# Table of filter stretches copied in 24 parts on SyncE's queue, one per image of attention; offsets loaded first, padded filters read back on ScalarE's queue

## The chip, the cores and the metric

The kernel runs on one core of one Trainium2 chip. The metric is device time in microseconds (us) of one execution; lower is better. The kernel before takes 10876.6 us, the median of 3 runs (10869.42 to 10882.96). A core has TensorE (PE in the views; PEld is its weight load), VectorE (DVE), ScalarE (ACT), GpSimd (POOL) and SyncE (SP), each with its own in-order stream of instructions, and 16 DMA engines. A DMA is issued by an instruction in the stream of SP, ACT or POOL ("SPq", "ACTq", "POOLq" in the views).

## The reference

Four layers, each of the form x = x + f(normalised x), over 32 images of 192 channels of 56 x 56:

```python
x = x + _L0_conv_ref(_gn(x), ...)   # agent attention, 6 heads, 49 agents
x = x + _L1_conv_ref(_gn(x), ...)   # a recurrent scan (RWKV) over the 3136 pixels
x = x + _L2_conv_ref(_gn(x), L2_conv_offset)   # shift by 48 offsets, 3x3 filter
x = x + _L3_conv_ref(_gn(x), L3_conv_z, ...)   # a long convolution
```

The part that the change touches belongs to the last layer. Its 192 filters of 55 x 55 don't depend on x; a small network of sines makes them from a position code z:

```python
h = jnp.sin(f1 * (einsum('bchw,oc->bohw', z, W1) + b1))
h = jnp.sin(f2 * (einsum('bchw,oc->bohw', h, W2) + b2))
k = einsum('bchw,oc->bohw', h, W3) * (jnp.exp(-distance_map * abs(deltas)) + shift)
y = irfft2(rfft2(x, s) * rfft2(k[0], s), s)[centre] + bias * x
```

and the third layer's 48 offsets are rounded to shifts, with a 3x3 filter for what is left.

## The kernel before, in words

**Stages.** `make_filter` makes the filters; `attention` does layer 0, image by image; `scan_pairs` does layer 1 on pairs of images; `channel_blocks` does layers 2 and 3 channel by channel, with the filters in a table in DRAM. Their order on each engine is made by a scheduler: it gives every instruction a place in its engine's stream, by its own model of times, and so instructions of neighbouring stages and images stand between each other. It can move a DMA issue ahead of code written earlier. What is put under `keep_in_program_order` is fixed behind the instruction that was traced last on the same engine.

**`make_filter`** loads z, weights and the distance map (L255), and calls `beside()`, which loads the first image and the weights of attention (L414 to L426). `_find_shifts` then loads the offsets `off` (L205) and positions `at` (L207), both on SP, and finds the shifts of layer 3 on VectorE (from L208). The sines are made in six rounds of matmul, seven VectorE instructions and one ScalarE instruction (L282 to L291); L317 and L319 make the filters `out` in two halves of 96 channels, and L324 stores each half in DRAM (`filt`). Eight DMAs (L335) write zeros to the ends of the table `lags`. Then six blocks of 32 channels follow: two DMAs read the block from `filt` into one of two `padded` tiles (L350, 55 rows, runs of 220 bytes), TensorE transforms its rows (L360), VectorE and ScalarE copy the result out in two forms, `straight` and `crossed` (L368 to L371), and eight DMAs write these to `lags` (L376, 55 x 8 runs of 336 bytes each). All of these DMAs are issued by SP.

**`copy_spans`** (L382) copies `lags` in DRAM to the table `spans` in DRAM, in the layout of `channel_blocks`: each DMA takes 16 channels and one of the two forms, 2352 KB, issued by GpSimd (L391). `attention` calls it as `beside(b)` for the first 12 images, two DMAs per call, 24 in all. Nothing in attention reads the result, so the scheduler is free to issue them early.

**`attention`**, for one image: statistics and pooled sums of the next image (`moments`: L504, L506, and `by_x`, L513), agents (L567 to L584), then four column groups j of the image. `seen` writes two small tables per image, `gk_c` and `gq_c`, by a DMA from a tile `once` that repeats it (L585, 597.2 KB each, on SP). In the first half `weigh` uses `gk_c` (L651, L652). Between the halves `ask` uses `gq_c`: matmuls L743 and L744 fill a tile in PSUM, VectorE finds a maximum (`mx`, L747) and subtracts it (`pq`, L748), which frees the PSUM tile; ScalarE takes the exponential (L756); VectorE sums and scales (L758 to L760). There are four PSUM tiles for all of it. `join` (L716 to L731) puts the four groups of the first half together, into `values`, with one small ScalarE exponential `f` (L719) in its midst. `turn_back` transposes (L770, copies L774), and `answer` multiplies by `values` (L783, L788). An image ends with stores (L880 to L885).

Tiles of `make_filter` and of attention share memory: the first `by_x` can be written only when the last `lags` DMA has read its source.

Of the kernel before, what the change touches and what calls it, by code (L numbers as in the profile page):

```python
# [20 lines left out]
F32 = mybir.dt.float32  # L21
# [7 lines left out]
C = 192  # L29
# [39 lines left out]
HALF = 64  # L69
FREQ = 2 * NF  # L70
LAGS = 2 * S
SPAN = 8
# [86 lines left out]
def _bc(ap, shape):  # L159

    return ap.unsqueeze(len(ap.shape)).to_broadcast(shape)
# [33 lines left out]
        return mean, rs, nb  # L195


def _find_shifts(nc, cp, a, k, taps):

    NP = C // 4
    found = cp.tile([128, NP, 12], F32, name="found", tag="found")
    off = cp.tile([128, NP, 2], F32, name="off", tag="off")
    nc.sync.dma_start(out=off, in_=a["L2_conv_offset"].partition_broadcast(128))  # L205
    at = cp.tile([128, 2], F32, name="at", tag="at")
    nc.sync.dma_start(out=at, in_=k["chan_k"][:, k["chan_k"].shape[1] - 2 :])  # L207
    nc.vector.tensor_scalar(off, off, -(2.0**21), 2.0**21, ALU.max, ALU.min)  # L208
    rnd = cp.tile([128, NP, 2], F32, name="rnd", tag="rnd")
    nc.vector.tensor_scalar(rnd, off, BIG, None, ALU.add)  # L210
    nc.vector.tensor_scalar(rnd, rnd, BIG, None, ALU.subtract)
    gs = cp.tile([128, NP * 2, 3], F32, name="gs", tag="gs")
    nc.vector.tensor_tensor(off, off, rnd, ALU.subtract)
    flat = off.rearrange("p n d -> p (n d)")
    for f in range(3):
        nc.vector.tensor_scalar(gs[:, :, f], flat, float(f - 1), None, ALU.add)
    nc.vector.tensor_tensor(gs, gs, gs, ALU.mult)
    nc.scalar.activation(gs, gs, AF.Exp, scale=-2.0)
    gsum = cp.tile([128, NP * 2], F32, name="gsum", tag="gsum")
    nc.vector.tensor_reduce(gsum, gs, AX.X, ALU.add)  # L220
    nc.vector.reciprocal(gsum, gsum)
    nc.vector.tensor_tensor(gs, gs, _bc(gsum, [128, NP * 2, 3]), ALU.mult)
    nc.vector.tensor_scalar(rnd, rnd, float(-S), float(S), ALU.max, ALU.min)

    ok, low = (cp.tile([128, NP], F32, name=n, tag=n) for n in ("ok", "low"))
    for i, axis in enumerate((1, 0)):
        nc.vector.tensor_scalar(ok, rnd[:, :, axis], at[:, i : i + 1], None, ALU.add)
        nc.vector.tensor_scalar(low, ok, -0.5, None, ALU.is_gt)
        nc.vector.tensor_scalar(ok, ok, S - 0.5, None, ALU.is_lt)
        nc.vector.tensor_tensor(ok, ok, low, ALU.mult)  # L230
        nc.vector.tensor_tensor(found[:, :, 6 * i : 6 * i + 3], gs[:, axis::2], _bc(ok, [128, NP, 3]), ALU.mult)
        for f in range(3):
            nc.vector.tensor_scalar(found[:, :, 6 * i + 3 + f], rnd[:, :, axis], float(1 - f), None, ALU.add)
    nc.sync.dma_start(out=taps, in_=found)
# [3 lines left out]
def make_filter(ctx: ExitStack, tc: tile.TileContext, a, consts, filt, lags, spans, taps, beside):  # L238
# [4 lines left out]
    nc = tc.nc  # L243
    cp = ctx.enter_context(tc.tile_pool(name="f_c", bufs=1))
# [6 lines left out]
    n = RC * KS  # L251

    def load(name, shape, ap):
        t = cp.tile(shape, F32, name=name, tag=name)
        nc.sync.dma_start(out=t, in_=ap)  # L255
        return t
# [8 lines left out]
    dist = load(  # L265
        "dist", [T, P2], a["L3_conv_distance_map"].rearrange("a b h w -> (a b h w)").partition_broadcast(T)
    )
    beside()
    _find_shifts(nc, cp, a, consts, taps)
    nd = cp.tile([T, 2], F32, name="nd", tag="nd")  # L270
    nc.vector.tensor_scalar(nd, per["deltas"], -1.0, None, ALU.mult)
    nc.vector.tensor_tensor(nd, nd, per["deltas"], ALU.min)
    out = cp.tile([T, 2, P2], F32, name="out", tag="out")
# [21 lines left out]
    for i in range(0, KS // RC, 2):  # L295
        p1 = pp.tile([128, BANK], F32, name="p1", tag="p1")
        for h in range(2):
            c = min(i + h, KS // RC - 1)
# [26 lines left out]


    NI = 16
    f1 = load("f1", list(consts["f1"].shape), consts["f1"])
    none = KH + 1
    zeros = cp.tile([T, (none + 1) * FREQ], F32, name="zeros", tag="zeros")  # L330
    nc.gpsimd.memset(zeros, 0.0)
    for t in range(2):
        for i in range(2):
            for r in (0, LAGS - none - 1):
                nc.sync.dma_start(  # L335
                    out=lags[t * T : (t + 1) * T, i, r : r + none + r % 2].rearrange("c r f -> c (r f)"),
                    in_=zeros[:, : (none + r % 2) * FREQ],
                )
    nc.sync.dma_start(out=spans[C * (S // SPAN) * 128 :], in_=zeros[0:SPAN, 0:FREQ])
    padded = [cp.tile([128, NI, HALF], F32, name=f"padded{i}", tag=f"padded{i}") for i in range(2)]  # L340
# [3 lines left out]
    def psum():  # L344
        return pp.tile([128, BANK], F32, name="ps", tag="ps")

    for c0 in range(0, C, 2 * NI):
        t = padded[c0 // (2 * NI) % 2]
        for i in range(2):
            nc.sync.dma_start(  # L350
                out=t[HALF * i : HALF * i + KS, :, 0:KS],
                in_=filt[c0 + i : c0 + 2 * NI : 2].rearrange("q (a b) -> a q b", b=KS),
            )
        flat = t.rearrange("p q w -> p (q w)")
        got = [wp.tile([128, NI // 2, 2, FREQ], F32, name=n, tag=n) for n in ("straight", "crossed")]
        for g0 in range(0, NI // 2, 3):
            n = min(3, NI // 2 - g0)
            ps = psum()
            for g in range(n):
                nc.tensor.matmul(  # L360
                    ps[:, g * 2 * FREQ : (g + 1) * 2 * FREQ], flat[:, (g0 + g) * 128 : (g0 + g + 1) * 128], f1,
                    start=True, stop=True,
                )
            cos, sin = (
                ps[:, : n * 2 * FREQ].rearrange("p (c m u) -> p c m u", m=2, u=NF)[:, :, m] for m in range(2)
            )
            a0, b0 = (x[:, g0 : g0 + n].rearrange("p g s (u m) -> p (g s) u m", m=2) for x in got)
            nc.vector.tensor_copy(a0[..., 0], cos)  # L368
            nc.scalar.copy(a0[..., 1], sin)
            nc.scalar.mul(b0[..., 0], sin, -1.0)  # L370
            nc.vector.tensor_copy(b0[..., 1], cos)  # L371
        for i, x in enumerate(got):
            for p in range(2):
                for s in range(2):
                    c = c0 + 2 * p + s
                    nc.sync.dma_start(  # L376
                        out=lags[c : c0 + 2 * NI : 4, i, none : none + KS].rearrange("g r f -> r g f"),
                        in_=x[HALF * p : HALF * p + KS, :, s],
                    )


def copy_spans(nc, lags, spans, c):  # L382


    n = S // SPAN
    for i in range(2):
        first = lags[c, i]
        there = bass.AP(first.tensor, first.offset, [[2 * LAGS * FREQ, 16], [SPAN * FREQ, n], [1, HALF * FREQ]])
        first = spans[c * n * 128 + HALF * i]
        here = bass.AP(first.tensor, first.offset, [[n * 128 * FREQ, 16], [128 * FREQ, n], [1, HALF * FREQ]])  # L390
        nc.gpsimd.dma_start(out=here, in_=there)  # L391


def _blocks_of(t, at):
# [4 lines left out]
class _Ready:  # L399
# [19 lines left out]
    def load(self, nc, a, k):  # L419
        self.first = self.image(nc, a, 0)  # L420
        for to, ap in ((self.k, k["att_k"]), (self.w, a["att_w"]), (self.c, a["att_c"])):
            nc.sync.dma_start(out=to, in_=ap)
        for to, ap in ((self.gk_c, a["coef_k"]), (self.gq_c, a["coef_q"])):
            nc.sync.dma_start(out=to[65:KC], in_=ap)
        for j, w in enumerate(WIDTHS):
            nc.sync.dma_start(out=self.xs_c[j][64:KC], in_=k["spread"][:, S * STARTS[j] : S * (STARTS[j] + w)])  # L426
# [1414 lines left out]
@with_exitstack  # L1841
def all_blocks(ctx: ExitStack, tc: tile.TileContext, a, k, out):
    nc = tc.nc
    NB = out.shape[0]
    dp = ctx.enter_context(tc.tile_pool(name="dram", bufs=1, space=DRAM))

    def scratch(name, shape):
        return dp.tile(shape, F32, name=name, tag=name)

    x1, x2 = scratch("x1", [NB, C, N]), scratch("x2", [C, 2, S, NB // 2, S])  # L1850
    filt, rs2 = scratch("filt", [C, KS * KS]), scratch("rs2", [C, 2, 2, NB // 2])
    lags, taps = scratch("lags", [C, 2, LAGS, FREQ]), scratch("taps", [128, C // 4, 12])
    spans = scratch("spans", [C * (S // SPAN) * 128 + SPAN, FREQ])
    st_a, st_c = scratch("st_a", [128, 2, NB // 2, 9]), scratch("st_c", [2, 64, 2, NB // 2, 9])
    with tc.tile_pool(name="a_r", bufs=1) as rp, tc.tile_pool(name="a_x", bufs=2) as xp:
        ready = _Ready(rp, xp)
        make_filter(tc, a, k, filt, lags, spans, taps, lambda: ready.load(nc, a, k))
        attention(
            tc, a, ready, x1, st_a, st_c, lambda b: copy_spans(nc, lags, spans, 16 * b) if b < C // 16 else None
        )  # L1860
    with tc.tile_pool(name="count", bufs=1) as cp:
        count = cp.tile([1, 1], I32, name="count", tag="count")
        scan_pairs(tc, a, k, x1, st_a, st_c, x2, rs2, count)
        n = nc.values_load(count[0:1, 0:1], min_val=0, max_val=128)
        with tc.If(n > 0):
            scan_guarded(tc, a, k, x1, x2, rs2)
    channel_blocks(tc, taps, k, x2, rs2, spans, out)
# [104 lines left out]
```

## Time and profile before

| What | us |
|---|---|
| median of 3 runs | 10876.6 |
| the profiled execution, its own time | 10882.12 |
| its span (first to last instruction) | 10880.3 |
| from the start to the first `by_x` of attention | 322.5 |
| store of one image to store of the next (L883, 656.74 to 803.32) | 146.6 |

Over the span TensorE is busy 88%, VectorE 85%, ScalarE 59%, GpSimd 27%. A page of the profile divides the span in 40 slices of 272 us: TensorE is at two tenths in the first and at nine in nearly all others, and the DMA engines at seven tenths in the first, one tenth through attention and eight to nine in the last quarter. In the views below, a line of waits names the waiting engine and line, what it waited for, and us in total, number of times, the longest. A line of the timeline starts with the start and the duration in us; the square brackets hold the idle time before it and what ended it.

### The profile page before, as it was taken

To read this page: it belongs to the slowest core of one execution; us is meant where nothing else is said; L and a number is where in the kernel's file an instruction comes from. 1 tells how busy PE (TensorE), PEld (TensorE's weight loads), DVE (VectorE), ACT (ScalarE), POOL (GpSimd) and SP (SyncE) were. 2 spreads that over 40 slices of the span, in tenths; PEclk is the share of its full clock that TensorE was granted. 3 is DMA by queue.
4 is the path that set the end of the run, shared out by engine and by line. 5 is a ranking of instruction groups with operands and counts; after the bars stand their busy time and mean duration, and the time that the engine had idled before them with its cause. 6 is when DMAs were issued, how large, how long until landed. Compare 5 with 4: busy or idle time off the path is not lost. (4 is left out here: it accounts for less than half of the span.)

```text
span 10880.3 us, 166788 instructions
## 1 busy us (share of the span) xinstructions
PE 9566.8 (88%) x64806; PEld 5949.0 (55%) x64806; DVE 9238.9 (85%) x11668; ACT 6379.6 (59%) x11966; POOL 2912.6 (27%) x2638
## 2 busy tenths in 40 slices
PE   2799999999999999998788888888888799999998
PEld 1456655555665555564333333333333578777776
DVE  2688888888888888887999999999999577777777
ACT  1455555555555555554666666666666476666666
POOL 0000000000000000001655555555555444444441
PEclk7899999999999999999899999999999899999999
DMA  7311111111111111112333444333333588988888
GB/s 226 121 39 31 43 45 45 45 45 35 35 44 45 45 45 45 31 37 63 82 97 99 100 98 101 102 99 97 97 97 99 152 273 272 274 273 272 275 269 265
DMA packets 1104878, 1240.32 MB, mean 114 GB/s; under 512 B 773091, under 2 KB 807200, under 8 KB 1091992
## 3 DMA queue, kind: packets, MB, share of 16 engines
q1 hardware_dynamic: 1090768, 1146.05, 37.1%
q0 software_dynamic: 3072, 57.80, 1.6%
q10 hardware_dynamic: 10240, 25.70, 0.9%
q8 instruction: 516, 8.45, 0.3%
q14 instruction: 282, 2.31, 0.1%
HBM read 915.94 MB, written 306.43 MB: 112 GB/s over the span
## 5 line engine op out<-in xcount | busy, mean ns | idle before, releaser
L638 DVE SCALAR_TENSOR_TENSOR o<-v_a,att_w,o 128x896 f32<-128x896 f32 (+1 forms) x1024 | 1054.6, 1030 | 422.5 <-ACT v_a L612 295.4
L1155 POOL MEMSET f<- 128x1 f32 x96 | 8.9, 99 | 4730.4 <-DMA st_c<-st 4725.2
L1535 DVE STREAM_TRANSPOSE z<-turned 128x1792 f32<-128x1792 f32 x192 | 677.7, 3529 | 275.9 <-ACT turned L1535 275.7
L1535 ACT COPY y<-ps 64x252 f32<-64x252 f32 (+1 forms) x2304 | 784.0, 340 | 159.8 <-PE ps L1535 130.3
L1148 ACT ACTIVATE q<-q 128x784 f32<-128x784 f32 x384 | 328.4, 855 | 810.5 <-DVE q L1143 635.4
L655 ACT ACTIVATE pr<-ps,low 98x896 f32<-98x896 f32 (+1 forms) x384 | 352.4, 918 | 560.0 <-DVE low L653 560.0
L903 PE MATMUL ps<-sq,fixed 128*128 128x392 f32 x512 | 298.2, 745 | 428.8 <-ACT sq L1226 428.8
L1535 POOL TENSOR_TENSOR xn<-x,scale 128x896 f32<-128x896 f32 x192 | 336.0, 1750 | 1194.9 <-DMA x<-x 704.2
L638 DVE SCALAR_TENSOR_TENSOR o<-v_c,att_w,o 128x448 f32<-128x448 f32 (+1 forms) x1024 | 635.9, 621 | 5.0
L651 PE MATMUL ps<-xs_a,gk_a 128*98 128x448 f32 (+1 forms) x1536 | 638.7, 496 | 0.0
L652 PE MATMUL ps<-xs_c,gk_c 125*98 125x448 f32 (+1 forms) x1536 | 633.3, 493 | 5.4 <-DMA gk_c<-once 5.4
L743 PE MATMUL ps<-gq_a,xs_a 128*112 128x294 f32 x1792 | 602.2, 417 | 19.2 <-DVE pq L748 19.2
L903 PE MATMUL ps<-x,weights 128*128 128x392 f32 x1536 | 573.2, 516 | 28.4 <-DVE bv L1177 14.3
L744 PE MATMUL ps<-gq_c,xs_c 125*112 125x294 f32 x1792 | 594.2, 412 | 0.0
L1535 PEld LDWEIGHTS ps<-toep,y 128*32 128x32 f32 x16896 | 515.0, 151 | 113.4 <-ACT y L1535 107.1
L1535 PE MATMUL ps<-toep,y 128*32 128x112 f32 x16896 | 562.5, 290 | 0.0
L756 ACT ACTIVATE pq<-pq 112x1176 f32<-112x1176 f32 x224 | 265.3, 1184 | 495.3 <-DVE pq L748 372.7
L1535 PE MATMUL ps<-rows,xn 128*112 128x112 f32 x3072 | 378.3, 281 | 151.2 <-POOL xn L1535 151.0
L1535 ACT ACTIVATE turned<-ps,rs 128x448 f32<-128x448 f32 (+1 forms) x576 | 383.5, 666 | 214.1 <-PE ps L1535 207.4
L1535 PE MATMUL ps<-fixed,padded 128*128 128x168 f32 x3072 | 493.5, 316 | 0.0
L1535 PEld LDWEIGHTS ps<-fixed,padded 128*128 128x128 f32 x3072 | 459.7, 197 | 2.4 <-issue 1.9
L903 PEld LDWEIGHTS ps<-sq,fixed 128*128 128x128 f32 x512 | 137.5, 285 | 579.7 <-ACT sq L1226 483.2
(369 smaller groups left out, 25658.8 us busy)
## 6 DMA issues: line engine op xcount, KB each, us to landing
toep<-spans SPq DMA_DIRECT2D x192, 2352.0 KB
x<-x SPq DMA_DIRECT2D x576, 392.0 KB
x<-x SPq DMA_DIRECT2D x896, 196.0 KB
out_x<-done SPq DMA_DIRECT2D x384, 196.0 KB
spans<-lags POOLq DMA_DIRECT2D x24, 2352.0 KB, 50.7
x<-in_x SPq DMA_DIRECT2D x32, 1568.0 KB
x<-x SPq DMA_DIRECT2D x32, 1568.0 KB
x<-in_x SPq DMA_DIRECT2D x64, 392.0 KB
```

The costliest lines, as they stand in the source:

```text
L638: nc.vector.scalar_tensor_tensor(dst, tap(i), dww[:, t, i : i + 1], dst, ALU.mult, ALU.add)
L651: mm(ps[P2, h, :n], g[:, cols], xs_a[j][:, px], start=True, stop=False)
L652: mm(ps[P2, h, :n], gk_c[0:KC, 2 * j + h, cols], xs_c[j][0:KC, px], start=False, stop=True)
L655: nc.scalar.activation(pr[:, :, :n], ps[P2, :, :n], AF.Exp, bias=low[:, j, p : p + 1], accum_out=sums[:, j, p : p + 1])
L743: mm(ps[:SUB, i, :HA], xs_a[j][:, px], g, start=True, stop=False)
L744: mm(ps[:SUB, i, :HA], xs_c[j][0:KC, px], gq_c[0:KC, 2 * j + (q + i) // ns], start=False, stop=True)
L756: nc.scalar.activation(flat, flat, AF.Exp)
L903: mm(out, aa, srcs[t][h], start=True, stop=False)
L1148: nc.scalar.activation(den, den, AF.Ln)
L1155: nc.gpsimd.memset(s, 0.0)
L1535: return lambda *args, **kw: self.tc.keep_in_program_order(do(*args, **kw))
```

## The change

Three edits. The offsets, the positions and the transform matrix `f1` are loaded ahead of `beside()`. The six reads of `filt` are issued by ScalarE instead of SP, two ahead of the loop and each later one behind the matmuls of the block that had the tile before. And `copy_spans` takes one part (16 channels, one form) per call, on SP, fixed in program order, for the first 24 images.

```diff
-    off = cp.tile([128, NP, 2], F32, name="off", tag="off")
-    nc.sync.dma_start(out=off, in_=a["L2_conv_offset"].partition_broadcast(128))
-    at = cp.tile([128, 2], F32, name="at", tag="at")
-    nc.sync.dma_start(out=at, in_=k["chan_k"][:, k["chan_k"].shape[1] - 2 :])
...
+    off = load("off", [128, C // 4, 2], a["L2_conv_offset"].partition_broadcast(128))
+    at = load("at", [128, 2], consts["chan_k"][:, consts["chan_k"].shape[1] - 2 :])
+    f1 = load("f1", list(consts["f1"].shape), consts["f1"])
     beside()
-    _find_shifts(nc, cp, a, consts, taps)
+    _find_shifts(nc, cp, off, at, taps)
...
-    for c0 in range(0, C, 2 * NI):
+    def fetch(c0):
         t = padded[c0 // (2 * NI) % 2]
         for i in range(2):
-            nc.sync.dma_start(
+            nc.scalar.dma_start(
...
+    fetch(0)
+    fetch(2 * NI)
+    for c0 in range(0, C, 2 * NI):
...
+        if c0 + 4 * NI < C:
+            fetch(c0 + 4 * NI)
         for i, x in enumerate(got):
...
-def copy_spans(nc, lags, spans, c):
+def copy_spans(tc, lags, spans, part):
     n = S // SPAN
-    for i in range(2):
-        first = lags[c, i]
...
-        nc.gpsimd.dma_start(out=here, in_=there)
+    c, i = 16 * (part // 2), part % 2
+    if c >= C:
+        return
+    first = lags[c, i]
...
+    tc.keep_in_program_order(tc.nc.sync.dma_start(out=here, in_=there))
...
-            tc, a, ready, x1, st_a, st_c, lambda b: copy_spans(nc, lags, spans, 16 * b) if b < C // 16 else None
+        attention(tc, a, ready, x1, st_a, st_c, lambda b: copy_spans(tc, lags, spans, b))
```

What it does to the order that the scheduler makes: on SP, `off`, `at` and `f1` stand ahead of the first image's load; the twelve `padded` reads are gone; the 48 `lags` writes stand in one row, then the second image's last load, then the first `spans` copy. In each of the first 24 images one `spans` copy stands between the loads of the next image and `gq_c`. On GpSimd the 24 copies are gone. Nothing of the work is added or taken away. But in the second to the 24th image the streams of TensorE, VectorE and ScalarE are changed too, around `ask` and `join`: on TensorE the first L743 of each of the four PSUM tiles of j = 0 stands ahead of all L744. On VectorE the small operations of `join` (`m`, `f`, `sums`, `den` and its reciprocal, `f` again) stand ahead of the first `mx` instead of between the fourth and the eighth, and `got` and `values` ahead of the fifth `mx` and `pq` instead of behind the seventh. On ScalarE the `f` of `join` comes ahead of the first exponential of `ask`. (On VectorE, the first image has this order of `join` and `ask` in the kernel before already.) From `scan_pairs` on, the order of every engine is the same.

More of the change, by code (lines that the diff above doesn't have):

```diff
@@ L195, in __call__, with _find_shifts @@
         return mean, rs, nb
-def _find_shifts(nc, cp, a, k, taps):
+def _find_shifts(nc, cp, off, at, taps):
     NP = C // 4
     found = cp.tile([128, NP, 12], F32, name="found", tag="found")
-    off = cp.tile([128, NP, 2], F32, name="off", tag="off")
-    nc.sync.dma_start(out=off, in_=a["L2_conv_offset"].partition_broadcast(128))
-    at = cp.tile([128, 2], F32, name="at", tag="at")
-    nc.sync.dma_start(out=at, in_=k["chan_k"][:, k["chan_k"].shape[1] - 2 :])
     nc.vector.tensor_scalar(off, off, -(2.0**21), 2.0**21, ALU.max, ALU.min)
@@ L327, in make_filter @@
     NI = 16
-    f1 = load("f1", list(consts["f1"].shape), consts["f1"])
     none = KH + 1
@@ L353, in make_filter @@
             )
+    fetch(0)
+    fetch(2 * NI)
+    for c0 in range(0, C, 2 * NI):
+        t = padded[c0 // (2 * NI) % 2]
         flat = t.rearrange("p q w -> p (q w)")
@@ L379, in make_filter @@
                     )
-def copy_spans(nc, lags, spans, c):
+def copy_spans(tc, lags, spans, part):
     n = S // SPAN
-    for i in range(2):
-        first = lags[c, i]
[L388 to L391, printed above, removed]
+    c, i = 16 * (part // 2), part % 2
+    if c >= C:
+        return
+    first = lags[c, i]
+    there = bass.AP(first.tensor, first.offset, [[2 * LAGS * FREQ, 16], [SPAN * FREQ, n], [1, HALF * FREQ]])
+    first = spans[c * n * 128 + HALF * i]
+    here = bass.AP(first.tensor, first.offset, [[n * 128 * FREQ, 16], [128 * FREQ, n], [1, HALF * FREQ]])
+    tc.keep_in_program_order(tc.nc.sync.dma_start(out=here, in_=there))
 def _blocks_of(t, at):
@@ L1857, in all_blocks @@
         make_filter(tc, a, k, filt, lags, spans, taps, lambda: ready.load(nc, a, k))
-        attention(
-            tc, a, ready, x1, st_a, st_c, lambda b: copy_spans(nc, lags, spans, 16 * b) if b < C // 16 else None
-        )
+        attention(tc, a, ready, x1, st_a, st_c, lambda b: copy_spans(tc, lags, spans, b))
     with tc.tile_pool(name="count", bufs=1) as cp:
```

## The prediction

> **What bounds the kernel now.** I read the page's slices first (TensorE is nearly idle in the first slice of 272 us, and the DMA engines are busiest there until the last stage), then the busy time by stretches of the start, then the waits of the first 600 us, then the timelines of SP and VectorE, and last one image of attention. Columns of the stretches: start and end, length, busy us of PE, PEld, DVE, ACT and POOL with instruction counts, granted clock, DMA share, GB/s.
>
> ```profile
> 134.04:162.72 28.68, 7.69 (x32) 6.61 (x32) 4.54 (x12) 3.72 (x12) 0.00 (x0) 0.62 0.70 142
> ...
> 200.00:220.00 20.00, 0.00 (x0) 0.00 (x0) 0.00 (x0) 0.00 (x0) 1.04 (x2) 0.50 1.01 333
> ...
> 345.00:4900.00 4555.00, 4375.34 (x24956) 2697.48 (x24954) 3936.26 (x5956) 2517.39 (x4494) 0.00 (x0) 0.98 0.15 42
> ```
>
> From 200 us no engine computes and the DMA engines are full; through attention (345 to 4900) TensorE is busy 96% and the DMA engines 15%. The waits tell what fills the start:
>
> ```profile
> POOL spans L391 <- DMA lags<-crossed: 171.3, 2, 113.5
> ...
> DVE by_x L513 <- DMA lags<-crossed: 136.0, 1, 136.0
> ...
> PE ps L360 <- DMA padded<-filt: 62.0, 3, 31.5
> ...
> DVE off L208 <- DMA off<-in_L_conv_offset: 19.3, 1, 19.3
> ```
>
> Three stalls end last, one after the other: 19.3 us for the offsets, 62.0 us for the filters read back, 136.0 us in which the first `by_x` waits for the last write of `lags`. Why that write is late is in the timeline:
>
> ```profile
> 184.94 4.15 POOL L391 DMA_DIRECT2D spans<-lags  x8
> ...
> 185.57 69.09 SPq L376 DMA_DIRECT2D lags<-crossed  x4
> ...
> 322.53 5.11 DVE L513 TENSOR_REDUCE by_x<-x 128x392 f32<-128x3136 f32 x2 [135.97 <-DMA lags<-crossed]
> ```
>
> GpSimd has put its copies of the table into the same DMA engines; the last four writes of 144.4 KB take 69 us to issue and land at 322.5. The copies are 57.8 MB (part 3, q0). At the 333 GB/s of 200 to 220 us that is 174 us of all DMA engines.
>
> **The sum, part by part**, against the profiled execution (10882.1 us, span 10880.3; the median of the runs is 5.5 us less).
>
> 1. *Offsets first.* VectorE's stream stands from 37.5 to 57.0 for `off`, and the sine chain with it. In the new order `off` is issued at about 3 us, right behind the distance map, which ScalarE has at 11.1; VectorE would want it at 9.3 and its next piece of the chain came at 11.1 anyhow. I keep 1.5 us of wait (bounds 0 and 4). The filters, ready at 89.3, are ready at 71.5.
> 2. *Read-back on ScalarE's queue.* No row shows a read here that isn't behind SP's writes. First block: 89.3 to the first `lags` write at 107.7 is 18.4 us, of which 5.8 is VectorE's statistics (L504, L506) that still stand ahead; so the first write is issued at 84 to 90, I take 87. Then 48 writes. Bounds: SP issues sixteen in 13.8 us (148.8 to 162.6), so 41 us for all if the rest hides; and 28.7 us for two blocks as now (134.04 to 162.72, above), 86 us, if nothing does. In that stretch the DMA engines' share is 0.70 already, partly with a copy of the table, so it is nearer to the upper end than issue alone says: 66 us. Last landing and `by_x` at 155 (bounds 130 and 175). The twelve issues now lie in ScalarE's stream, where the copies of L369 and L370 are queued behind them; SP's issues of this read took 0.4 to 3.2 us, and ScalarE is busy 3.7 of the 28.7 us, so this hides while lags are limited by transfers; without that cover it is up to 12 x 1.6 = 19 us, inside the bounds.
> 3. *Copies out of the way.* 322.5 to 155 is 167.5 us (150 to 195). Behind `by_x`, `gk_c` is issued at 339.5 and its matmul waits 5.4 us to 356.5 beside four table copies; with one copy of 7 us ahead of it that wait goes. Sum of the start: 172 us less.
> 4. *The 24 copies in attention.* Each is 2.4 MB, 7.2 us of all DMA engines (174 / 24), in images of 146.6 us at 15% share. On SP it stands behind the loads of the next image and ahead of `gq_c`:
>
> ```profile
> 813.74 0.92 SPq L585 DMA_DIRECT2D gq_c<-once  x1
> ```
>
> Its first use is the L744 behind the first L743 at 863.6, so 50 us of cover; loads (2.35 MB, 7 us), copy and the 17 us that `gk_c` took from issue to use in the crowded start end 30 us after issue. I cost it at nothing; behind `gq_c` in SP's stream comes `gk_c` 119 us later.
> 5. *The order of `ask` and `join`.* In 23 images VectorE now does `join` before the first `mx`, and `got` and `values` before the fifth. VectorE works without a gap there, and TensorE waits for it through the PSUM tiles:
>
> ```profile
> 870.23 0.75 DVE L747 TENSOR_REDUCE mx<-ps 112x12 f32<-112x588 f32 x1
> ...
> 885.44 0.76 DVE L748 TENSOR_TENSOR pq<-ps,mx 112x588 f32<-112x588 f32 x1
> ```
> ```profile
> 885.59 4.69 PE L770 MATMUL ps<-att_k,pq 112*98 112x112 f32 x24 [2.52 <-DVE f L724]
> ...
> 890.32 2.45 PE L783 MATMUL ps<-pqT,values 98*64 98x448 f32 x8
> ```
>
> The seventh `pq` starts at 885.44, and the transposes L770 start as the sixth ends. Laid out with these durations in the new order: `m`, `f`, ScalarE's `f` (0.21), `sums`, `den`, reciprocal, `f` put the first `mx` from 870.2 to 871.6; up to the sixth `pq`, `got` (0.34 and 0.94) and `values` (1.48 and 0.29) come in addition, about 2.7 us; the sixth `pq` ends at 889.2 instead of 885.4, and L770 and L783 come 3.8 us later. Behind it the exponential of the seventh and eighth `pq` now stands behind the three copies of L774, so VectorE's sum waits for it. The first image shows that, as it has this order already: there VectorE waits 1.90 us for ScalarE at 452.1, and from L783 to the first L903 it is 449.97 to 465.88, 15.9 us, against 890.32 to 905.05, 14.7. From L903 to the store both take 44.5 to 44.9 us: nothing is made up. So 3.8 + 1.2, less what TensorE's own slack takes back: I take 4.3 us. Bounds: 1.4 us (the whole stretch from the first L743 to L903 in that first image is 42.9 us against 41.5; but VectorE was free there when the first tile came) and 5.5. 23 x 4.3 = 99 us (32 to 127).
>
> Sum: 10882.1 - 172 + 99 = 10809, and 5.5 less for the median: **10804 us**. With the bounds, 10882.1 - 195 + 32 and 10882.1 - 150 + 127, both less 5.5: 10714 to 10854.
>
> A rule on step 2. The row: the share of 0.70 in the stretch with two blocks of writes and reads, though every engine waits for DMA. The Trainium skill, page "DMA: Bandwidth & Descriptors", section "Why a DMA increments its semaphore by 16 and not by 1", says that a transfer runs on the largest number of DMA engines up to 16 that divides its outer dimension. By it the 55 rows of these reads and writes use 11 of 16, a share of 0.69, which the row agrees with; the stretch would then be full already, six blocks would take near the upper bound of 86 us, and the sum would be 20 us higher.
>
> **The rivals.**
>
> *The order costs nothing:* VectorE's permuted work sums to the same, and waits elsewhere shrink. For it: the 1.4 us of the first image. Against: VectorE had slack there and has none at 870 to 899. 10882 - 172 - 5 = 10705 us. Chance 0.17.
>
> *The start stays slow:* reads and writes of the filter, now in flight together, slow each other, ScalarE's stream is held by its issues, and `by_x` comes at 220 or so (half of 322.5 - 155 less 20 for the offsets). For it: the share of 0.70. Against: no table copies are left in it. 10882 - 105 + 99 - 5 = 10871. Chance 0.10.
>
> *The table's copy holds up `gq_c` (slower):* on SP's queue, copy and `gq_c` share one line. Part 6 has for the copy a median of 50.7 us from issue to landing:
>
> ```profile
> spans<-lags POOLq DMA_DIRECT2D x24, 2352.0 KB, 50.7
> ```
>
> If a copy took that in attention, `gq_c` would land at 813.7 + 8 + 50.7 + 11 = 883, 20 us behind its use: 24 x 20 = 480 us, 10882 - 172 + 99 + 480 - 5 = 11284. It makes the kernel slower from 3 us per image (172 - 99 over 24). Against: that median comes from up to ten copies in line at full DMA engines. Chance 0.06.
>
> *The change doesn't do what it says:* a copy floats early again, or `by_x` waits for the first copy too. The new order has each copy between the loads and `gq_c`, so 0.04; 10870.
>
> **How the numbers follow.** The forecast has 0.63. From 10700 to 10855 lie it and the first rival, 8 in 10. A difference of 0.2% (22 us) is about what a measurement can tell from no change: faster is below 10855, slower above 10898. Faster 0.83 (forecast, first rival, a part of the second), same 0.09, slower 0.08.
>
> **What would show it.** Steps 1 to 3: no wait of VectorE for `off` above 4 us, first `by_x` between 130 and 175. Step 4: no wait of L743 or L744 for a DMA. Step 5: from the second image on, store to store near 151 us up to the 24th image and 146.6 behind; L770 waiting for VectorE some 6 us instead of 2.5. Wrong would be the forecast if `by_x` came after 200, or if images 2 to 24 took 146.6.

## The result, and the profile after

The changed kernel takes **10802.0 us**, the median of 4 runs (10796.5 to 10811.1), where the kernel before took 10873.0 beside it (4 runs, 10864.6 to 10883.0). The ratio is 0.9935, 95% interval 0.9918 to 0.9952: 71 us less. The profiled execution took 10811.1 us with a span of 10809.3.

Where the 71 us are, from the two profiled executions (store: SP's issue of the first store of an image, L883 before and L891 after; attention's lines are 8 higher in the changed kernel):

| Point | before, us | after, us | gained so far |
|---|---|---|---|
| first `by_x` | 322.5 | 160.0 | 162.5 |
| store of the 1st image | 510.4 | 346.3 | 164.1 |
| store of the 24th image | 3885.7 | 3820.1 | 65.7 |
| store of the 32nd image | 5044.3 | 4982.6 | 61.7 |
| end of the span | 10880.3 | 10809.3 | 71.0 |

The start gives 164 us. The 23 images behind it give 98.4 back: store to store is 151.03 us on average, 146.75 before, 4.28 each. Another 4.0 goes in the last eight images. The last 9.3 us, from the last store to the end, are no effect of the change: this stretch is the same program in all kernels of this study, and it took 5815 to 5836 us in their profiles (5836.0 in the kernel before; 5835.6 and 5815.4 in the two profiled executions of experiment 1's kernel, 10713.8 and 10694.8 us, whose last stores of attention are only 1.1 us apart).

**The start.** Busy time by stretches (columns as in the prediction's first view), the start up to `by_x` and then attention:

```profile
0.00:160.00 160.00, 67.03 (x192) 40.74 (x192) 68.52 (x209) 35.44 (x66) 9.12 (x13) 0.84 0.73 181
180.00:4840.00 4660.00, 4420.31 (x24962) 2712.91 (x24958) 3953.38 (x5956) 2512.78 (x4495) 0.00 (x0) 0.97 0.17 52
```

The same 192 matmuls of the start now lie in 160 us. Attention is TensorE's still, but its share fell from 96% to 95% while it got the DMA engines' 57.8 MB more. The waits of the first 100 us on VectorE, then those of the first 420 us:

```profile
DVE off L204 <- DMA off<-in_L_conv_offset: 2.2, 1, 2.2
```
```profile
PE ps L364 <- DMA padded<-filt: 21.3, 1, 21.3
...
DVE by_x L521 <- DMA x<-in_x: 7.5, 1, 7.5
```

The three stalls of before, 19.3, 62.0 and 136.0 us, are 2.2, 21.3 and 7.5. (The last names the load that was last on SP's queue; `by_x` waits for the last writes of `lags` before it, and in experiment 8 the same wait is put down to them.) The 62.0 were three waits for the reads; one is left, and it is longer than the first of the three was (13.0). SP's queue shows why:

```profile
48.91 9.02 SPq L333 DMA_DIRECT2D lags<-zeros  x5
59.92 0.94 SPq L323 DMA_DIRECT2D filt<-out  x1
60.91 2.49 SPq L333 DMA_DIRECT2D lags<-zeros  x1
72.40 0.30 SPq L323 DMA_DIRECT2D filt<-out  x1
72.75 5.49 SPq L333 DMA_DIRECT2D lags<-zeros  x2
91.61 0.27 SPq L337 DMA_DIRECT2D spans<-zeros  x1
...
99.31 3.32 SPq L382 DMA_DIRECT2D lags<-straight  x4
...
150.87 3.85 SPq L382 DMA_DIRECT2D lags<-crossed  x4
...
156.80 0.63 SPq L399 DMA_DIRECT2D spans<-lags  x1
```

The second half of the filters is stored at 72.4 (89.3 before), but the first write of `lags` comes only at 99.3. The first five zero fills (`lags<-zeros`) stand otherwise than before: in the kernel before SP had issued them by 67.8, 9 us ahead of the first store, here it ends them at 57.9, just ahead of it. The first store of before:

```profile
76.81 0.30 SPq L324 DMA_DIRECT2D filt<-out  x1
```

The 48 writes take 55.4 us, and the first copy of the table comes behind them.

**An image of attention.** TensorE from the last tile of the first column group to the transposes, 4th image:

```profile
729.46 0.66 PE L752 MATMUL ps<-gq_c,xs_c 125*112 125x294 f32 x2
733.20 1.84 PE L542 MATMUL ps<-mv,att_k 128*128 128x1 f32 x8 [3.08 <-DVE pq L756]
735.23 4.36 PE L778 MATMUL ps<-att_k,pq 112*98 112x112 f32 x24 [0.19 <-DVE pq L756]
```

L542 is the small matmul for the next image's normalisation, ahead of the transposes. Before, it ran without a wait and the transposes waited 2.5 us (the line at 885.59 in the prediction):

```profile
882.09 0.98 PE L534 MATMUL ps<-mv,att_k 128*128 128x1 f32 x8
```

Now it is the first that needs the PSUM tile which VectorE's late `pq` frees: 3.08 us. Over the 23 images the waits show this line, and none for a DMA:

```profile
PE ps L542 <- DVE pq L756: 70.9, 23, 3.1
```

VectorE in that image, its first maximum and the sixth and seventh `pq`:

```profile
717.55 0.76 DVE L755 TENSOR_REDUCE mx<-ps 112x12 f32<-112x588 f32 x1
...
734.33 1.43 DVE L756 TENSOR_TENSOR pq<-ps,mx 112x588 f32<-112x588 f32 x2
```

Counted from the first L751 of the image (709.43), the first `mx` starts after 8.1 us and the sixth `pq` ends after 25.6; in the kernel before it was 6.7 and 21.9.

### The profile page after: what moved, and what is told of

It reads as the page before. It is cut to its first block, busy times and chain, and to the rows that moved or that the text cites. A ratio compares the mean times of both kernels' runs of the same rounds, so it can differ in the third digit from the quotient of the medians.

```text
span 10809.3 us, 166766 instructions
## 1 busy us (share of the span) xinstructions
PE 9604.3 (89%) x64806; PEld 5959.0 (55%) x64806; DVE 9260.0 (86%) x11668; ACT 6372.8 (59%) x11964; POOL 2918.0 (27%) x2614
## 5 line engine op out<-in xcount | busy, mean ns | idle before, releaser
L751 PE MATMUL ps<-gq_a,xs_a 128*112 128x294 f32 x1792 | 609.0, 422 | 46.6 <-DVE pq L756 24.1
L1543 PE MATMUL ps<-rows,xn 128*112 128x112 f32 x3072 | 378.5, 281 | 159.6 <-POOL xn L1543 136.0
L766 DVE TENSOR_REDUCE sm<-pq 112x24 f32<-112x1176 f32 x224 | 307.7, 1374 | 181.9 <-ACT pq L764 181.9
```

What stands on the lines that cost most here:

```text
L751: mm(ps[:SUB, i, :HA], xs_a[j][:, px], g, start=True, stop=False)
L766: nc.vector.tensor_reduce(sm, rows, AX.X, ALU.add)
L1543: return lambda *args, **kw: self.tc.keep_in_program_order(do(*args, **kw))
```

## The experiments

The kernels ran in four groups, each beside runs of the kernel before (median 10872.1 us in the first group, 10879.6 in the second, 10874.2 and 10876.4 in the last two). Theory: the start gains what the copies held up, and VectorE's order in 23 images takes 98 us back. Its rival: the copies' traffic in attention takes it.

**1. The copies behind `gq_c`.**

```diff
-        beside(b)
...
                 gq = seen(ag, wqT, gq_c, "gq_a")
+                beside(b)
```

> The changed kernel with one call moved: each of the 24 copies of the table is issued on SP's queue right behind the transfer of gq_c instead of right ahead of it. Nothing else differs, and VectorE's program is again the order of the kernel before: in images 2 to 24 m<-low stands behind the fourth mx, not ahead of the first. Theory (order): the 98 us that 23 images lost, 4.3 us each, came from VectorE's order alone; store to store is 146.7 us again, the start keeps its 164 us, so 10802 - 98 = 10704 us (10690 to 10720). Rival (traffic): the 2.4 MB copies in attention cost the 4.3 us, whatever VectorE's order: 10802 us, store to store 151.

10702.5 us (10688.6 to 10718.6, 5 runs), ratio 0.9844 (0.9830 to 0.9857). In SP's stream this moves each copy by one transfer, 0.9 us: `gq_c` is issued at 645.76 in the 4th image and the copy at 646.74. The place of the call decides how the scheduler arranges VectorE. TensorE, same point of the 4th image:

```profile
713.67 0.66 PE L752 MATMUL ps<-gq_c,xs_c 125*112 125x294 f32 x2
714.16 0.98 PE L542 MATMUL ps<-mv,att_k 128*128 128x1 f32 x8
717.66 4.69 PE L778 MATMUL ps<-att_k,pq 112*98 112x112 f32 x24 [2.52 <-DVE f L732]
```

That is the kernel before again, wait for wait (2.52 at the transposes), with the whole traffic of the copies still there. From the 1st to the 24th store it takes 146.7 us per image, and the last store is at 4876.4, 168 us ahead of before. Run once more beside the last experiments it took 10695.4 us, ratio 0.9847 (0.9831 to 0.9864).

> The kernel with the copies behind gq_c once more, beside the run with earlier zero fills: 10702 us (10690 to 10715).

**2. One channel of sixteen ahead of `gq_c`, fifteen behind.**

```diff
-        beside(b)
+        beside(b, 0)
...
                 gq = seen(ag, wqT, gq_c, "gq_a")
+                beside(b, 1)
...
+    c, m = (c + 1, 15) if late else (c, 1)
```

> As the run before, but a sixteenth of each copy (one channel of 16) stays on SP's queue ahead of gq_c, and fifteen sixteenths go behind it. The same bytes are moved in the same images; VectorE's order is the changed kernel's in images 2 to 24. Theory (order): 10802 us like the changed kernel (10790 to 10815), store to store 151.0 with a wait of about 3 us of TensorE at L542's counterpart for pq. Rival (place or traffic ahead of gq_c): with almost nothing ahead of gq_c the loss is gone, 10704 us.

10798.1 us (10781.1 to 10801.6, 5 runs), ratio 0.9926 (0.9912 to 0.9939): the changed kernel's time, with almost all bytes where experiment 1 had them. In this kernel attention's lines stand one higher:

```profile
728.96 1.84 PE L543 MATMUL ps<-mv,att_k 128*128 128x1 f32 x8 [3.08 <-DVE pq L757]
730.99 4.39 PE L779 MATMUL ps<-att_k,pq 112*98 112x112 f32 x24 [0.19 <-DVE pq L757]
```

The 3.08 us are back, in 23 images, and TensorE waits for no DMA there. 1 and 2 differ in the place of 147 KB per image and in the order of VectorE, TensorE and ScalarE that follows from it, and by 96 us. So the order costs them, not the traffic.

**3. Twice the traffic, order of before.**

```diff
     tc.keep_in_program_order(tc.nc.sync.dma_start(out=here, in_=there))
+    tc.keep_in_program_order(tc.nc.sync.dma_start(out=here, in_=there))
```

> The copies behind gq_c as in the first run, each issued twice (the second writes the same values again), so 4.7 MB per image instead of 2.35; VectorE's order is that of the kernel before. Theory (traffic in attention is covered): 10704 us as without the second copy (up to 10712: one more issue in the start, where the last read of gk_c shares the DMA engines with it). Rival (traffic costs 4.3 us per copy): 24 x 4.3 = 103 us above the first run.

10717.8 us (10689.6 to 10726.5, 4 runs), ratio 0.9860 (0.9845 to 0.9876). The median is 6 us above the expected range; the interval overlaps that of experiment 1, and the rival's 103 us are excluded. The profile is finer: store to store over the images with copies is 146.87 us where experiment 1 has 146.74, so the second copy costs 3 us in 23 images, not 103, and the last store comes at 4871.3, where experiment 1 has 4876.4. Attention hides 4.7 MB per image but for these 0.13 us; the prediction's step 4 holds with a margin of one more copy.

**4. The copies on GpSimd's queue, at the place of the change.**

```diff
-    tc.keep_in_program_order(tc.nc.sync.dma_start(out=here, in_=there))
+    tc.keep_in_program_order(tc.nc.gpsimd.dma_start(out=here, in_=there))
```

> The changed kernel with the copies on GpSimd's queue instead of SP's, at the same place of the program; VectorE's order is that of the kernel before. Theory (order): 10704 us, store to store 146.7. Rival (the copy's traffic ahead of gq_c): 10802. A third case, that GpSimd's queue issues its copies early, since GpSimd does nothing else in attention: the copies crowd together in the first images and the start, by_x comes later than 160 us, and the time is 20 to 170 us above 10704.

10858.2 us (10845.3 to 10865.2, 11 runs), ratio 0.9986 (0.9977 to 0.9995). The third case came, 154 us above 10704 and so within its range: the order is kept among GpSimd's own instructions only, and GpSimd has nothing to do. GpSimd, and the first wait of VectorE:

```profile
151.81 4.39 POOL L399 DMA_DIRECT2D spans<-lags  x8
166.20 0.52 POOL L399 DMA_DIRECT2D spans<-lags  x1 [10.00 <-DMA spans<-lags]
```
```profile
DVE by_x L521 <- DMA x<-in_x: 153.2, 1, 153.2
```

Eight copies are issued within 4.4 us, ahead of the last writes of `lags`, and `by_x` comes at 306.9. Store to store is 146.8 us, as in the kernel before. This is the changed kernel with its first two edits whole and the third without effect in the start: 15 us (5 to 25), of the 170 that experiment 1 has.

**5 to 7. Each edit alone.** The diffs are the three parts of the change; in 7 the copies stand behind `gq_c`, so that VectorE's order is the one of before.

> The kernel before with the first edit alone: the offsets, the grid row and f1 are loaded ahead of the images. Prediction's step 1: the filters are stored 17.8 us earlier (71.5 instead of 89.3) and everything behind comes as much earlier, 10872 - 18 = 10854 us. Theory now (zero fills): the writes of zeros, 5 of lags and one of spans, filled the DMA engines while VectorE waited for the offsets; with that wait gone they stand ahead of the filters, the read-back starts at about 92 as in the changed kernel, and the first write of lags is issued at about 99 instead of 107.7: 8 to 9 us less, 10863 us.

> The kernel before with the second edit alone: the filters are read back on ScalarE's queue, two blocks ahead; the copies are still GpSimd's, behind each 32 channels of lags. Theory (the copies set the start): the writes of lags are issued without SP's wait for the reads, but the copies, 57.8 MB or 174 us at 333 GB/s, are then in the same DMA engines all the earlier, and the last write of lags still lands behind most of them: by_x at 280 to 320, 5 to 40 us less, 10832 to 10867 us. Rival (the reads in SP's line set the start): 48 writes in 55 us behind 107, by_x at 170, so 150 us less, 10722 us.

> The kernel before with the third edit alone, its copies issued on SP's queue behind gq_c's transfer in 24 images (VectorE's order as in the kernel before). Theory (the copies set the start): no copy is left among the writes of lags; the filters come at 89.3, the first write at 107.7, and six blocks follow of 18 to 25 us each (28.7 with copies among them), with reads on SP between them: by_x at 215 to 255, 70 to 105 us less: 10770 to 10800 us. Rival (it is the three edits only together): by_x stays near 300 and the time within 30 us of 10872.

| Kernel | median, us | ratio (95%) | first `by_x` | last store of attention |
|---|---|---|---|---|
| before | 10872 to 10880 | 1 | 322.5 | 5044.3 |
| 5, offsets alone | 10856.9 | 0.9984 (0.9975 to 0.9993) | 319.4 | 5038.1 |
| 6, read-back alone | 10859.5 | 0.9984 (0.9975 to 0.9993) | 310.0 | 5030.5 |
| 4, both, copies early | 10858.2 | 0.9986 (0.9977 to 0.9995) | 306.9 | 5025.2 |
| 7, copies alone | 10725.2 | 0.9868 (0.9853 to 0.9883) | 181.3 | 4896.7 |
| 1, all three | 10702.5 | 0.9844 (0.9830 to 0.9857) | 161.1 | 4876.4 |

In 5 the first write of `lags` comes at 99.2 instead of 107.7, as the theory of the zero fills had it, but the copies leave only 3.1 us of that at `by_x`. In 6 `by_x` is in the range of the theory (280 to 320), and the rival's 170 is out. In 7 the rival (that nothing but the three together helps) is out. The third edit alone is worth 144 us (127 to 160), more than the 105 at the far end of my expectation. With the copies still on GpSimd the first two, each by itself, bring 6 and 14 us at the last store; their time of 17 us has an interval of 8 to 27, and I can't tell more from it. 20 us of the whole are theirs once the copies are away (181.3 to 161.1). In 7 I had expected six blocks of 18 to 25 us. SP shows that they are far shorter once no copy lies between:

```profile
107.23 2.63 SPq L376 DMA_DIRECT2D lags<-straight  x4
...
134.97 2.70 SPq L376 DMA_DIRECT2D lags<-straight  x4
...
172.86 3.40 SPq L376 DMA_DIRECT2D lags<-crossed  x4
```

Between these rows stand four reads each time, for two blocks; two blocks take 27.7 us (107.2 to 135.0), so 13.9 each, and `by_x` comes at 181.3. My expectation took 28.7 us for one block where the kernel before had written two in it; that was a slip of the expectation. What is worth keeping is the pace of a pair of blocks, reads and writes in one line on SP: 27.7 us without a copy. In the kernel before the first pair took 41.1 us (107.7 to 148.8), with 1.8 copies' packets among its own; the second took 27.2 (148.8 to 176.0), as by then the two first copies were nearly through (a fifth of one is left behind 134.0). It was the later copies, eight and more in line, that held up the last four writes.

**8 to 10. Why the first write of `lags` is late.** All three are experiment 1 with the nine zero fills (eight of `lags`, one of `spans`) at another place: behind the load of `f1`; behind the first image's loads; or, tied to the last block by one row, behind all writes of `lags`. The diffs show the new places in this order:

```diff
     f1 = load("f1", list(consts["f1"].shape), consts["f1"])
+    none = KH + 1
...
+    nc.sync.dma_start(out=spans[C * (S // SPAN) * 128 :], in_=zeros[0:SPAN, 0:FREQ])
     beside()
```
```diff
     beside()
+    none = KH + 1
...
+    nc.sync.dma_start(out=spans[C * (S // SPAN) * 128 :], in_=zeros[0:SPAN, 0:FREQ])
     _find_shifts(nc, cp, off, at, taps)
```
```diff
                         in_=x[HALF * p : HALF * p + KS, :, s],
                     )
+    nc.gpsimd.tensor_scalar(zeros[:, 0:FREQ], got[1][0:T, 0, 0], 0.0, None, ALU.mult)
+    for t in range(2):
+        for i in range(2):
+            for r in (0, LAGS - none - 1):
...
+    nc.sync.dma_start(out=spans[C * (S // SPAN) * 128 :], in_=zeros[0:SPAN, 0:FREQ])
```

> The kernel with the copies behind gq_c (10702.5 us), and the zero fills of lags and spans issued right behind the load of f1, ahead of the images' loads, instead of between the two stores of the filters. Theory (zero fills): the DMA engines are free when the second filter is stored; the read-back starts at about 76 instead of 92, the first write of lags at 84 to 88 instead of 99, by_x at 145 to 150 instead of 160: 10 to 14 us less, 10689 to 10693 us. Rival (the DMA engines are full of loads anyway): the loads are late instead, and it stays at 10702.

> As the kernel with the copies behind gq_c, with the zero fills issued right behind the first image's loads (ahead of the write of taps), so that they neither delay those loads, as the fills ahead of them did, nor stand between the two stores of the filters. Theory (zero fills): they are through the DMA engines at about 65 to 70; the read-back of the filters starts at 76 to 80 instead of 92, by_x comes at 148 to 154 instead of 160, 6 to 12 us less than the same kernel without this edit on this chip. Rival (the start is bounded by the DMA engines' total work): the second image's loads, which now stand ahead of the writes of lags, take the place of the fills, and nothing is gained (within 5 us).

> The kernel with the copies behind gq_c, and the zero fills tied to the last block of the read-back (one row of the zeros is made from it, multiplied by 0), so that they stand behind all writes of lags; the second image's loads move ahead of the stores of the filters. This run tells what delayed the first write of lags (99.3 us where 87 was predicted), not how to be faster: the fills then hold up by_x at the end. Theory (zero fills): nothing is queued in the DMA engines when the second filter is stored at about 72; the read-back starts within 5 us, TensorE's first transform at 80 to 84 instead of 93.1, the first write of lags at 85 to 90 instead of 99.3; by_x at 160 to 170. Rival (store and read-back themselves take that long): the first transform stays at 91 to 95 though nothing else is in the DMA engines.

The two earlier places failed: 10708.3 us (0.9849, 0.9836 to 0.9863) and 10708.2 us (0.9848, 0.9835 to 0.9861), `by_x` at 166.0 and 169.4. The fills left, and what they had pushed back came in their place: the image loads then stood right behind the stores of the filters, and the first write of `lags` came at 104.3 and 108.2. These two runs could not tell the cause. The last one could (10721.2 us, 0.9859, 0.9839 to 0.9879). TensorE, SP and VectorE in it:

```profile
75.09 3.70 PE L356 MATMUL ps<-f,padded 128*128 128x168 f32 x12 [3.76 <-DMA padded<-filt]
```
```profile
84.14 3.28 SPq L374 DMA_DIRECT2D lags<-straight  x4
...
142.25 15.52 SPq L382 DMA_DIRECT2D lags<-zeros  x8
```
```profile
171.51 3.42 DVE L522 TENSOR_REDUCE by_x<-x 128x392 f32<-128x3136 f32 x1 [32.07 <-DMA spans<-zeros]
```

With nothing queued at the store of the filters, the first transform starts at 75.1 instead of 93.1 and the first write at 84.1 instead of 99.3. So the fills (with the load that follows them) made it late. But at the end they hold up `by_x` for 32 us, and nothing is won: in none of the three does `by_x` come earlier than in experiment 1. That fits a start bounded by the DMA engines' whole work; that it is so was not tried by itself, and their share over the first 160 us of the changed kernel is 0.73, so they are not full all the time.

## Why the prediction was right, point by point

10804 us was forecast, 10802.0 was measured. The path was the forecast one: the start gains, and the order of `ask` and `join` gives back in 23 images what step 5 said. Two terms of the start were mis-sized in opposite directions. That the numbers agree to 2 us is luck: the start came 7.9 us short and the last eight images lost 4.0, while the last stage was 9.3 us shorter in the profile and the median lay 9.1 us below the profiled execution where 5.5 were taken.

1. *Offsets first.* Right: wait 2.2 us (1.5 taken, bounds 0 and 4), filters stored at 72.4 (71.5 forecast).
2. *Read-back.* The first write was to come at 84 to 90, 87 taken; it came at 99.3. The step that failed is that the stretch from the store to the first write was carried over from the kernel before (18.4 us, or 12.6 without VectorE's statistics); it took 26.9. The zero fills are not in it: in the kernel before five of them were issued by 67.8, in and behind VectorE's wait for `off` and 9 us ahead of the first store, and step 1 moved that store to 59.9, right behind them. Without the fills, and with the second image's loads ahead of the store, the write comes at 84.1 (experiment 10); with step 1's edit alone it comes at 99.2 (experiment 5). The 48 writes were to take 66 us (bounds 41 and 86); they take 55.4, or 58.0 in experiment 10. The value was leaned towards the upper bound, 28.7 us for each two blocks, because the DMA engines' share was 0.70 there, "partly with a copy"; but only a fifth of a copy is in that stretch. Experiment 7 shows what the bound is: 27.7 us with no copy near it, 13.9 of them between the last write of a pair and the first of the next, in which SP issues the reads and no write can start before they are back. With the reads off SP the writes are nearer to the lower bound. The writes began 12 us late and took 11 us less; from their last issue to `by_x` it was 5.3 us where 2 had been left, and `by_x` came at 160.0, 155 forecast. Of ScalarE's twelve issues the first four took 13.8 us, from 78.0 on, while ScalarE had nothing else to do; the other eight took 0.3 to 1.3 us each and hid.
3. *Copies out of the way.* 162.5 us at `by_x` where 167.5 was forecast, and the start in all 164.1 where 172 was (bounds 150 and 195; from the bounds of `by_x`, 130 and 175, they are 147.5 and 192.5, which changes nothing here). Of the 5.4 us that were to go with the wait for `gk_c`, the wait did go and 1.6 us came: from `by_x` to the store 187.9 became 186.3. TensorE's granted clock (the column ahead of the DMA share) shows a likely cause. Before, the 35 us that begin 22.5 us behind `by_x`:

```profile
345.00:360.00 15.00, 9.61 (x25) 3.73 (x24) 11.87 (x15) 8.43 (x15) 0.00 (x0) 0.86 0.63 207
360.00:380.00 20.00, 18.18 (x77) 9.24 (x76) 10.45 (x12) 8.62 (x17) 0.00 (x0) 0.93 0.14 31
```

and after, those that begin 20 us behind it:

```profile
180.00:195.00 15.00, 15.00 (x28) 5.04 (x25) 5.93 (x7) 9.06 (x16) 0.00 (x0) 0.50 0.00 0
195.00:215.00 20.00, 17.61 (x69) 8.65 (x68) 15.46 (x19) 8.27 (x15) 0.00 (x0) 0.96 0.14 31
```

28 matmuls fill the 15 us at a clock of 0.50, where 25 had taken 9.6 at 0.86; the two L618 from 185.83 on take 1.70 us together, and their counterparts of before, the two L610 from 346.90 on, took 0.92. The transfer is no longer late, but the clock is: it is at 1.00 only from 36.4 us behind `by_x` on. Other kernels of this study that start nearly as early, without a wait for `gk_c`, got it back at other times. In experiments 1 and 3 it was after 26.5 to 26.9 us, and from `by_x` to the store it took 181.0 to 181.3 us; in experiments 8 and 9 it was after 39.0 and 39.2 us, and it took 188.1 and 189.1. So in experiment 1 the 5.4 us came in full (6.6), and here the later clock took 5 of them back. No run sets the clock by itself; why the grant comes later in one kernel than in another stays open.

4. *The copies in attention cost nothing.* Right: no wait for `gq_c`, and experiment 3 hides twice as much. The rival that it is held up took its price, 50.7 us from issue to landing, from copies that stood in line. Spread over the images, the data of a copy is through 12.6 to 14.9 us after its issue (2nd to 24th image).
5. *The order.* Right in size: 4.3 us forecast, 4.28 measured (store to store 151 as forecast), 99 and 98.4 us for 23 images. The rival at nothing fell with experiments 1 and 2. Its stretch was right too: from the first L743 to the transposes it is 25.8 us against 22.0, 3.8 as laid out, and the sixth `pq` ends where step 5 had put it. One sign was misplaced: the transposes were to wait 6 us for VectorE, and it is L542 ahead of them that takes the wait (3.08), as it needs the tile first; with the 0.19 of the transposes it is half of the 6. Behind the transposes, over the 23 images, TensorE is 0.65 us later at L903 and 0.16 of it is made up by the store, where 1.2 less TensorE's slack was laid out: 3.80 + 0.65 - 0.16 = 4.29. The 4.0 us of the last eight images were not forecast. Three of them take 149.1 to 149.3 us; images of 149.2 us stand in the kernel before too (the 10th and the 23rd), but none among its last eight. What makes them is open.

*The page's rule*, that a transfer runs on the largest number of DMA engines up to 16 that divides its outer dimension (the Trainium skill, "DMA: Bandwidth & Descriptors", section "Why a DMA increments its semaphore by 16 and not by 1"): the prediction drew from it a ceiling of 11 of 16, 0.69, on these transfers of 55 rows, and 86 us on the six blocks. From 131 to 154 us of the changed kernel only writes of `lags` (q1) and reads of the filters (q10) travel:

```profile
q1 hardware_dynamic: 10487, 3.44, 82.1%
q10 hardware_dynamic: 920, 0.20, 4.5%
```

86.6% of 16 engines, and 55.4 us: the ceiling does not hold, and the 0.70 of before is no sign of it. The number of engines for one transfer is not refuted by that. The twelve reads, of 880 runs each, left 10692 packets on q10 (60 to 160 us), 11 for each beside its runs; the 24 copies of the kernel before, with 16 rows outside and 112 runs each, left 3072, 16 for each beside its runs. These are the numbers that the rule gives. What failed is the step from 11 engines for a transfer to a ceiling for several in flight. Whether other engines take part then or packets of one engine overlap in the profile's times, no run tells; for 5% of this stretch it counts 17 packets or more at once, and the copies' share in the prediction's first view is 1.01, so such a share does not count engines.

## What to carry to other kernels

Before a stall is removed, list what runs in its shadow: the zero fills were out of the way while VectorE waited for the offsets, and stood right ahead of the filters once it didn't. Where a scheduler arranges the engines, compare the order of every engine, not only of the one that is edited: leaving a sixteenth of a copy one transfer earlier on SP changed VectorE's order in 23 images and cost 96 us (experiments 1 and 2), two thirds of the 144 that the copies' move brings alone. Price such a reorder from the tile that the bottleneck waits for, and then look for a place of the same instruction that leaves the order alone.

## What the runs showed of the hardware that was not expected

The granted clock can take back a gain: with TensorE's start 162 us earlier, 28 matmuls ran without a gap at 0.50 for 15 us where the kernel before had 0.86 soon behind its `by_x`, and kernels with nearly the same start got the clock of 1.00 back 26.5 to 39.2 us behind `by_x`. A transfer of 2.35 MB per image is free in attention (DMA share 0.17), and a second one costs 0.13 us, while the same bytes issued in a row cost 141 us at `by_x` (181.3 against 322.5). And the program order that holds a DMA on SP, whose queue is paced by other transfers, holds nothing on an idle engine: GpSimd issued eight copies in 4.4 us.
